# Down products by sevens in an MLP whose weights are unpacked on the way

## The chip, the cores and the metric

The kernel runs on one core of a Trainium2 chip. The metric is the device time of one execution in microseconds (us). Engines are named as in the profile: PE (TensorE, matrix products; PEld is its loading of weights), DVE (VectorE), ACT (ScalarE), POOL (GpSimd) and SP (SyncE, which here only issues DMAs).

## The reference

Two sequences of T = 1024 tokens with model width DM = 512 pass through two layers, everything in fp32. Each layer adds an attention and then an MLP to x, both on a layer norm of x: `x = x + attn0(ln(x)); x = x + mlp0(ln(x)); x = x + attn1(ln(x)); x = x + mlp1(ln(x))`. Attention 0 is a gated delta rule (a recurrence over tokens, computed in chunks of 128 tokens); attention 1 is a softmax attention through a small latent. MLP 0, where most of the change lies, has its weights as 4-bit codes with one scale for 32 values:

```
Wg = dequant(gate_W_packed, gate_scales)      # 4096 x 512, Wu alike; Wd 512 x 4096
gate, up = xt @ Wg.T, xt @ Wu.T
inter = gelu(gate) * up                       # tokens x 4096
out = inter @ Wd.T
```

MLP 1 is sparse (two of four hidden values are kept) and isn't touched.

## The kernel before

**Stages.** The two sequences are worked on half a step apart. `weave(main, fill)` (L157) interleaves the instructions of two generators: main says at each yield how much filling it wants (FILL = 3.3), fill says how much it has given (STEP = 3.4, or half of it for one product of seven). In the stage that the change acts in, main is the delta attention of sequence 1 (`delta.second`, 8 chunks of 128 tokens) and fill is MLP 0 of sequence 0 (`Unpacked.rest`). In the stage after it main is attention 1 of sequence 0 and fill is MLP 0 of sequence 1 (`Second.run`). The instruction order of PE, DVE, ACT and POOL is the order in which the program issues them; each engine works strictly through its own list. SP issues the DMAs in the same way.

**MLP 0, sequence 0 (`Unpacked`).** The 4096 hidden units are cut into NC0 = 8 chunks of 512. For each chunk six units of weights have to be unpacked: gate, up and down, each in halves. A unit (`unpack`) is three jobs: two times three DVE operations (two on the integer codes, L925 and L926, and a scaling product, L929), and then, for the gate and up units, four sums on POOL (L229 to L232), the store of the unpacked weights to DRAM (`kept`, for sequence 1) and the load of the codes of the unit two places further on (`codes.load`: one DMA of codes and eight of scales, L910 and L914). `plan` puts the jobs of units into a queue, and `core.spend(n)` issues n of them.

Chunks 0 and 1 (EARLY = 2) are done in plain products. In chunks 2 to 7 the gate and up products are done "by sevens": a 2 x 2 block product in seven block products instead of eight (`SEVEN`, in the order 1, 2, 6, 5, 7, 3, 4), with sums of blocks as factors (S1, S2, S3, S4 on the left from `left_sums`, T1 to T4 on the right from `right_sums`). One such set is a `macro`: seven products of two 128x512 matmuls (L1018). Products 1, 6 and 5 are copied out of PSUM by ACT into a tile `part` (L991), the others are added or multiplied in by DVE (L1036, L1048, L1052), and the second addend is put on with one product's delay. Two PSUM banks take the products in turn. An fp32 matmul is two rows in the profile's counts.

The down products of chunks 2 to 7 were plain: `outcome` goes over the 8 token tiles, multiplies four 128x512 matmuls into one bank (`o_ps`, the matmul itself is in a helper, L201), has DVE add the bank to x (L1161) and spends one unpacking job per tile. Jobs are also spent at each product of a macro. The order of units in later chunks was gate 0, up 0, down 0, gate 1, up 1, down 1: each macro planned one unit, and the down stretch two.

**MLP 0, sequence 1 (`Second`).** It reads the unpacked weights back, and does all three products by sevens, the down products too (`Seven.output`, `right_factors`, `left`; matmuls of 128x256, L1064, x adds L1079 on DVE and L1081 on POOL). Its pool of weights (`z_left`, two buffers) is opened in `open()`, after the first weave has ended, and its first weights are asked for there.

**x of sequence 0** is eight tiles of 128x512 (`Core.hold`), stored to DRAM (`park`, L1163) as each is finished in the last chunk. Attention 1's weights (L1369 to L1378) are loaded into the place of x, and its first work is to read the parked x back (`xl`, L1441).

**Delta attention, sequence 1.** Each chunk passes through `early` (prepare, solve), `late` (invert, advance) and `normed`. `fetch` loads its stored projections `cv` (a ring of 2) and its gate `gw` (a ring of 3) one slot ahead. The triangular inverse is a run of small DVE operations (`prod` L603, `inv` L604); `Ud` L693 and `o` L724 follow from PE results.

Of the kernel before, what the change touches and what calls it, by code (L numbers as in the profile page):

```python
# [81 lines left out]
class Core:  # L82
# [21 lines left out]
    def hold(self, pool, b):  # L104

        for n in range(b * TT, (b + 1) * TT):
            self.x[n] = pool.tile([P, DM], F32, tag=f"x{n}", name=f"x{n}")
# [146 lines left out]
class Delta:  # L254
# [570 lines left out]
    def second(self, stored, away, fill):  # L825
# [5 lines left out]
        def fetch(c):  # L831
            d = self.d[c]
            d["cv"] = self.ring("cv", [P, 3 * NG, P], 2)
            nc.sync.dma_start(out=d["cv"], in_=self.away[c][0])
            d["gw"] = self.ring("gw", [P, NH, DH], 3)
            nc.sync.dma_start(out=d["gw"], in_=self.away[c][1])
            d["beta"], d["g"] = self.late[:, c, :NH], self.late[:, c, NH:]
# [7 lines left out]
        def early(c):  # L845
            if c < CH:
                yield from self.prepare(c)
                yield
                yield
                yield from self.solve(c)  # L850

        def late(c):
            if 0 <= c < CH:
                x = self.d[c]["x"] = self.ring("x", [P, DM], 2)
                nc.sync.dma_start(out=x, in_=a["x"][(CH + c) * P : (CH + c + 1) * P, :])
                yield from self.invert(c)
# [16 lines left out]
        for slot in range(CH + 2):  # L873
            if slot + 1 < CH:
                fetch(slot + 1)
# [84 lines left out]
class Seven:  # L960
# [122 lines left out]

    def places(self, x, q):
# [7 lines left out]
class Unpacked(Seven):  # L1092
# [6 lines left out]
    def __init__(self, core, banks, codes, xT, kept, park):  # L1099
        super().__init__(core, banks, AF.Gelu_apprx_tanh, core.nc.vector)  # L1100
        self.codes, self.xT, self.kept, self.park = codes, xT, kept, park
# [4 lines left out]
        later = (("gate", 0), ("up", 0), ("down", 0), ("gate", 1), ("up", 1), ("down", 1))  # L1106
# [4 lines left out]
    def tile(self, u):  # L1111
# [3 lines left out]
        if w == "down":  # L1115
            t = self.wp.tile([P, 2, 512], F32, tag="w_down", bufs=3, name="w_down")
# [37 lines left out]
    def outcome(self, c, hs, tbs):  # L1154
# [3 lines left out]
        for n in range(4 * tbs[0], 4 * tbs[-1] + 4):  # L1158
            po = self.banks.one("o_ps")
            product(nc, po, [(h, wd[s // 2][:, s % 2, :]) for s, h in enumerate(hs(n))])  # L1160
            nc.vector.tensor_add(core.x[n], core.x[n], po)  # L1161
            if c + 1 == NC0:
                nc.sync.dma_start(out=self.park[n], in_=core.x[n])  # L1163
            core.spend(3 - len(tbs))
            yield STEP

    def chunk(self, c, tb, swap=None):
# [14 lines left out]
        if swap:  # L1182
            swap()
            self.plan(c + 1, ("gate", 0), ("up", 0))
        elif tb:
            self.plan(c + 1, ("gate", 1), ("up", 1), ("down", 0), ("down", 1))
        yield from self.outcome(
            c, lambda n: [h[:, s, n % 4 * P : n % 4 * P + P] for s in range(4)], (tb,)
        )
# [19 lines left out]
    def macro(self, c, half, w, g):  # L1209

        left = self.blocks(self.ws.pop((c, w, half)))
        for p in self.gate(left, g) if w == "gate" else self.up(left, g):
            self.step(p, 0)
            self.core.spend(1)
            yield STEP / 2
        self.core.spend()

    def rest(self):
# [5 lines left out]
        for c in range(self.EARLY, NC0):  # L1224
            gs = [self.wp.tile([P, 2, 2, T // 2], F32, tag=f"h{half}", name="h0") for half in range(2)]
            for (half, w), ahead in zip(
                ((0, "gate"), (0, "up"), (1, "gate"), (1, "up")),
                (("down", 0), ("gate", 1), ("up", 1), ("down", 1)),
            ):
                self.plan(c, ahead)  # L1230
                yield from self.macro(c, half, w, gs[half])
            self.step(4, 0)
            self.plan(c + 1, ("gate", 0), ("up", 0))
            yield from self.outcome(
                c,
                lambda n: [gs[s // 2][:, s % 2, n // 4, n % 4 * P : n % 4 * P + P] for s in range(4)],
                (0, 1),
            )
            core.spend()
# [3 lines left out]
class Second(Seven):  # L1243
# [4 lines left out]
    def __init__(self, core, banks, xT, x, kept, park):  # L1248
        super().__init__(core, banks, AF.Gelu_apprx_tanh, core.nc.gpsimd)
        self.x, self.kept, self.park = x, kept, park  # L1250
        self.tokens(xT, core.pools("g_x"), core.nc.vector)

    def open(self):
        self.wp = self.core.pools("g_w")
        self.tmp = self.core.pools("g_tmp")
        self.todo = [(c, w, half) for c in range(NC0) for half in range(2) for w in ("gate", "up")]
        self.ws = {self.todo[0]: self.weights(self.todo[0])}
        self.sums(self.todo[0])

    def weights(self, u):  # L1260
# [3 lines left out]
        t = self.wp.tile([P, 7, 2 * P], F32, tag="z_left", bufs=2, name="z_left")  # L1264
# [20 lines left out]
    def right_factors(self, wd):  # L1285
        half = DM // 2
        blocks = {
            f"{i + 1}{j + 1}": wd[:, 2 * i : 2 * i + 2, j * half : (j + 1) * half] for i in range(2) for j in range(2)
        }
        new = [self.wp.tile([P, 2, half], F32, name=f"wd_t{i}") for i in range(2, 5)]  # L1290
# [869 lines left out]
```

## Time and profile before

| | us |
|---|---|
| median of three runs | 3184.75 |
| lowest, highest | 3184.72, 3187.76 |
| profiled execution | 3184.22 |
| its span | 3182.5 |

The span is the stretch from the first to the last instruction of the profiled execution; some 1.7 us lie around it. Four windows of the trace give the stages (us; busy time of each engine in it, and the clock that the throttle granted to PE):

| window | length | PE | DVE | ACT | POOL | clock |
|---|---|---|---|---|---|---|
| 0 to 520: attention 0 of both, first MLP tokens | 520 | 462.18 | 365.15 | 202.90 | 139.88 | 0.94 |
| 520 to 1292: delta of sequence 1, MLP 0 of sequence 0 | 772 | 756.54 | 417.40 | 155.00 | 164.84 | 0.99 |
| 1292 to 2210: attention 1 of sequence 0, MLP 0 of sequence 1 | 918 | 909.88 | 570.54 | 307.99 | 279.64 | 0.99 |
| 2210 to the end: the rest | 972.5 | 952.04 | 609.84 | 267.25 | 155.19 | 0.98 |

A group's line in the profile reads: source line, engine, operation, output <- inputs by the program's names, shape, count | busy us, mean ns of one | idle time of the engine just before them, and what ended it. "<-DVE part L1052" behind an idle time means that the engine waited for that DVE operation. Matmuls overlap, so the mean ns of one is more than the pace from start to start. The chain of waits lists start, duration and what it was.

### The profile page before, as it was taken

How to read it: one execution, taken by the hardware profiler on the slowest of the kernel's cores; microseconds unless marked ns; L12 is line 12 of the kernel's file. 1: busy time of each engine (PE TensorE's matmuls, PEld its weight loads, DVE VectorE, ACT ScalarE, POOL GpSimd, SP SyncE). 2: the span in 40 equal slices, each digit the busy share in tenths (PEclk: the TensorE clock that was granted, in tenths of full speed). 3: DMA queues.
4: the chain of work that ended last, by engine and by line, in shares of the span. 5: the costliest groups of instructions: out<-in, count | busy, mean ns of one | idle time of the engine just before them, and what ended most of it. 6: DMA issues, size and time to landing. Idle time of an engine off the chain costs nothing.

```text
span 3182.5 us, 35790 instructions
## 1 busy us (share of the span) xinstructions
PE 3080.6 (97%) x13012; PEld 1624.7 (51%) x13012; DVE 1962.9 (62%) x3609; ACT 933.1 (29%) x1380; POOL 739.5 (23%) x790
## 2 busy tenths in 40 slices
PE   7899899999999999999999999999999999999998
PEld 6788654555555554454444354346433233334547
DVE  6787753366666555357567575655575577454766
ACT  4544311122121211221354114622202710442221
POOL 3333201122222211346312121222100700340000
PEclk9999999999999999999999999999999999999999
DMA  2111134132322224236301211123000020015211
GB/s 91 35 30 29 51 98 148 43 109 90 106 87 84 91 81 161 67 121 207 113 25 53 71 48 37 47 77 119 27 30 11 4 77 14 1 66 166 70 47 50
DMA packets 194784, 229.15 MB, mean 72 GB/s; under 512 B 53744, under 2 KB 148464, under 8 KB 194096
## 3 DMA queue, kind: packets, MB, share of 16 engines
q1 hardware_dynamic: 194608, 226.86, 22.3%
q8 instruction: 103, 1.69, 0.2%
q14 instruction: 73, 0.60, 0.1%
HBM read 154.16 MB, written 72.61 MB: 71 GB/s over the span
## 4 chain that ended last, share of the span: by engine, by line
PE 76%; DVE 5%; POOL 2%; issue 2%; DMA 1%; ACT 1%; SPq 0%; DVEq 0%; POOLq 0%; ACTq 0%
PE z_ps L1018 24%; PE o_ps L201 12%; PE z_ps L1064 8%; PE u_ps L201 5%; PE g_ps L201 5%; PE st_ps L1562 5%; PE av_ps L1593 4%; PE s_ps L1504 4%; PE den_ps L1615 1%; PE wide_ps L640 1%; PE small_ps L630 1%; PE hT_ps L1405 1%; PE small_ps L201 1%; PE wide_ps L397 1%; PE wide_ps L558 1%
## 5 line engine op out<-in xcount | busy, mean ns | idle before, releaser
L991 ACT COPY part<-z_ps 128x512 f32<-128x512 f32 x288 | 168.5, 585 | 738.3 <-PE z_ps L1018 501.5
L1018 PE MATMUL z_ps<-xT,z_left 128*128 128x512 f32 x768 | 359.7, 598 | 0.1
L1513 DVE TENSOR_REDUCE top<-s_ps 128x2 f32<-128x1024 f32 x256 | 301.0, 1217 | 77.5 <-PE s_ps L1504 77.4
L1018 PE MATMUL z_ps<-xt,z_left 128*128 128x512 f32 x576 | 274.9, 600 | 2.2 <-issue 1.0
L1573 ACT ACTIVATE es<-st_ps 128x1024 f32<-128x1024 f32 x214 | 209.9, 1022 | 129.5 <-PE st_ps L1562 124.4
L1018 PEld LDWEIGHTS z_ps<-xT,z_left 128*128 128x128 f32 x768 | 141.3, 190 | 187.6 <-issue 162.5
L201 PE MATMUL o_ps<-w_down,h 128*128 128x512 f32 x512 | 230.0, 600 | 0.4 <-DVE part L1052 0.4
L1018 PE MATMUL z_ps<-xT,w_left 128*128 128x512 f32 x384 | 182.0, 603 | 3.7 <-DVE part L1052 2.7
L1052 DVE TENSOR_TENSOR part<-z_ps,part 128x512 f32<-128x512 f32 x108 | 74.4, 689 | 174.1 <-PE z_ps L1018 168.5
L1018 PEld LDWEIGHTS z_ps<-xt,z_left 128*128 128x128 f32 x576 | 106.4, 191 | 147.3 <-issue 124.9
L1608 POOL TENSOR_TENSOR es<-es 128x512 f32<-128x512 f32 x96 | 132.5, 1408 | 148.5 <-PE av_ps L1593 144.9
L1562 PE MATMUL st_ps<-q,kT 17*128 17x512 f32 x1024 | 162.0, 657 | 1.7 <-ACT es L1573 1.7
L1504 PE MATMUL s_ps<-kT,q 16*128 16x512 f32 x1024 | 154.2, 640 | 4.9 <-DVE top L1513 4.8
L201 PEld LDWEIGHTS o_ps<-w_down,h 128*128 128x128 f32 x512 | 95.4, 191 | 110.7 <-issue 106.3
L201 PE MATMUL proj_ps<-xT,wqkv 128*128 128x256 f32 x576 | 135.2, 389 | 14.4 <-ACT gw L427 14.4
L1593 PE MATMUL av_ps<-es,v 128*32 128x512 f32 x1024 | 141.9, 626 | 0.0
L1018 PE MATMUL z_ps<-xt,w_left 128*128 128x512 f32 x288 | 137.8, 601 | 0.7 <-DVE part L1052 0.7
L1635 DVE TENSOR_TENSOR acc<-acc,es 128x1024 f32<-128x1024 f32 x96 | 131.8, 1420 | 0.0
L1053 POOL TENSOR_TENSOR h<-h,part 128x512 f32<-128x512 f32 x48 | 66.5, 1387 | 279.9 <-DVE part L1052 279.9
L201 PEld LDWEIGHTS proj_ps<-xT,wqkv 128*128 128x128 f32 x576 | 108.4, 193 | 33.6 <-ACT gw L427 17.6
L1036 DVE TENSOR_TENSOR h<-z_ps,part 128x512 f32<-128x512 f32 x84 | 57.9, 689 | 102.4 <-PE z_ps L1018 89.4
L1161 DVE TENSOR_TENSOR x<-x,o_ps 128x512 f32<-128x512 f32 x64 | 43.9, 686 | 122.3 <-PE o_ps L201 122.2
(316 smaller groups left out, 5317.0 us busy)
## 6 DMA issues: line engine op xcount, KB each, us to landing
sums<-factor SPq DMA_DIRECT2D x24, 512.0 KB, 3.4
kept_gate<-w_left SPq DMA_DIRECT2D x12, 896.0 KB, 3.8
kept_up<-w_left SPq DMA_DIRECT2D x12, 896.0 KB, 3.9
z_left<-kept_gate SPq DMA_DIRECT2D x12, 896.0 KB, 4.6
z_left<-kept_up SPq DMA_DIRECT2D x12, 896.0 KB, 4.5
kept_down<-w_down SPq DMA_DIRECT2D x16, 512.0 KB, 3.0
wd<-kept_down SPq DMA_DIRECT2D x16, 512.0 KB, 4.1
xl<-park SPq DMA_DIRECT2D x32, 256.0 KB, 2.9
```

The lines of the kernel that those rows point to most:

```text
L201: nc.tensor.matmul(ps, lhsT, rhs, start=(i == 0), stop=(i == len(pairs) - 1))
L991: self.core.nc.scalar.copy(t, src)
L1018: self.core.nc.tensor.matmul(ps, left[l][:, k, :], self.right[r][:, k, :], start=(first and k == 0), stop=(k == 1), skip_group_check=True,)
L1052: nc.vector.tensor_add(v, ps, v)
L1064: nc.tensor.matmul(ps[:, i * dm : (i + 1) * dm], left[l][:, k, i * P : (i + 1) * P], right[r][k], start=(first and i == 0 and k == 0), sto ...
L1504: nc.tensor.matmul(tiles[h4 // 2][:, h4 % 2 * 512 : h4 % 2 * 512 + 512], q1s[t][r : r + HALF, gr, :], kT[r : r + HALF, gr, j * 512 : (j + ...
L1513: nc.vector.tensor_reduce(top[:, j, h : h + 2], tiles[e].rearrange("p (i k) -> p i k", i=2), AX.X, ALU.max, negate=True)
L1562: nc.tensor.matmul(tiles[h4 // 2][h4 % 2], kT[r : r + CR, gr, kt * P : (kt + 1) * P], q2[r : r + CR, gr, :], start=True, stop=True,)
L1573: nc.scalar.activation(t.rearrange("p i q -> p (i q)"), tile[2], AF.Exp, scale=HALF**-0.5)
L1593: nc.tensor.matmul(av[gr][32 * h4 : 32 * h4 + 32, :], v[:, kt, 4 * gr + h4, :], es[u][h4 // 2][:, h4 % 2, :], start=(kt == 0), stop=(kt == ...
L1608: eng.tensor_add(t, t, es[u][h4 // 2][:, h4 % 2, :])
L1635: nc.vector.tensor_add(t, es[u - 1][e] if kt == 1 else t, es[u][e])
```

## The change

The down products of chunks 2 to 7 in `Unpacked` are done by sevens (`outputs`): two halves q of the tokens, each with seven products of four 128x256 matmuls, with left factors summed on DVE, right factors on POOL, three copies on ACT, and the x adds on DVE and POOL. No unpacking job is spent in them. Therefore the units come in the order gate 0, up 0, gate 1, down 0, up 1, down 1, and the four macros of a chunk plan one, two, two and one of them. A chunk's two down halves lie in one tile `wd`. The four right sums begin at product 3 of the last macro. x of sequence 0 becomes one tile of 128 x 8 x 512, since a place of an x add spans two token tiles, and its parks go out in two lots. In `Second` the pool for `z_left` is one of its own, opened with the object, and the first weights are asked for there. Delta's rings become one `cv` and two `gw`; the next `cv` is fetched after the first step of `prepare`, and `gw` in `late`.

```diff
@@ Core.hold
-        for n in range(b * TT, (b + 1) * TT):
-            self.x[n] = pool.tile([P, DM], F32, tag=f"x{n}", name=f"x{n}")
+        x = pool.tile([P, TT, DM], F32, name="x")
+        for n in range(TT):
+            self.x[b * TT + n] = x[:, n, :]
+        return x
@@ Delta.second
-            d["cv"] = self.ring("cv", [P, 3 * NG, P], 2)
+            d["cv"] = self.ring("cv", [P, 3 * NG, P], 1)
             nc.sync.dma_start(out=d["cv"], in_=self.away[c][0])
-            d["gw"] = self.ring("gw", [P, NH, DH], 3)
-            nc.sync.dma_start(out=d["gw"], in_=self.away[c][1])
...
-                yield from self.prepare(c)
+                steps = self.prepare(c)
+                next(steps)
+
+                if c + 1 < CH:
+                    fetch(c + 1)
+                yield
+                yield from steps
...
+                gw = self.d[c]["gw"] = self.ring("gw", [P, NH, DH], 2)
+                nc.sync.dma_start(out=gw, in_=self.away[c][1])
                 yield from self.invert(c)
...
-            if slot + 1 < CH:
-                fetch(slot + 1)
@@ Seven (moved here from Second)
+    def right_factors(self, wd, pool):
...
+        new = [pool.tile([P, 2, half], F32, tag=f"wd_t{i}", bufs=1, name=f"wd_t{i}") for i in range(2, 5)]
+        right = right_sums(self.core.nc.gpsimd, blocks, new)
...
+    def left(self, hs, q, calls, pool, again=False):
...
+        names = (1, 2) if again else (1, 2, 4)
+        new = [pool.tile([P, 2, HB], F32, tag=f"h_s{i}", bufs=1, name=f"h_s{i}") for i in names]
+        if again:
+            new.append(blocks["12"])
+        return left_sums(Recorder(self.core.nc.vector, calls), blocks, new)
@@ Unpacked
-        later = (("gate", 0), ("up", 0), ("down", 0), ("gate", 1), ("up", 1), ("down", 1))
+        later = (("gate", 0), ("up", 0), ("gate", 1), ("down", 0), ("up", 1), ("down", 1))
...
-        if w == "down":
-            t = self.wp.tile([P, 2, 512], F32, tag="w_down", bufs=3, name="w_down")
+        if w == "down" and c + 1 < self.EARLY:
+            t = self.plain.tile([P, 2, 512], F32, tag="w_down", name="w_down")
+        elif w == "down":
+
+            if half == 0:
+                self.wd = self.wp.tile([P, 4, 512], F32, tag="wd", name="wd")
+            t = self.wd[:, 2 * half : 2 * half + 2, :]
...
@@ Unpacked.macro
             self.core.spend(1)
+            if p == 3 and (half, w) == (1, "up"):
+                self.factors = self.right_factors(self.wd, self.sevens)
             yield STEP / 2
         self.core.spend()
+
+    def outputs(self, c, gs):
+
+        core, nc = self.core, self.core.nc
+        calls = deque()
+        left = self.left(gs, 0, calls, self.sevens, True)
+        for q in range(2):
+            for p in self.output(left, self.factors, self.places(self.x, q), nc.gpsimd):
+                self.step(p, 0)
+                if p == 1:
+                    while len(calls) > 1:
+                        calls.popleft()()
+                elif p == 6:
+                    calls.popleft()()
+                elif p == 4 and q == 0:
+                    left = self.left(gs, 1, calls, self.sevens, True)
+                elif p == 2 and q == 1:
+                    self.keep(c, 0)
+                yield STEP / 2
+        if c + 1 == NC0:
+            self.step(4, 0)
+            self.step(4, 0)
+            self.keep(c, 1)
+
+    def keep(self, c, q):
+
+        if c + 1 == NC0:
+            for n in (2 * q, 2 * q + 1, 4 + 2 * q, 5 + 2 * q):
+                self.core.nc.sync.dma_start(out=self.park[n], in_=self.core.x[n])
@@ Unpacked.rest
-                (("down", 0), ("gate", 1), ("up", 1), ("down", 1)),
+                (
+                    ((c, "up", 0),),
+                    ((c, "gate", 1), (c, "down", 0)),
+                    ((c, "up", 1), (c, "down", 1)),
+                    ((c + 1, "gate", 0),),
+                ),
             ):
-                self.plan(c, ahead)
+                for u in ahead:
+                    self.plan(u[0], u[1:])
                 yield from self.macro(c, half, w, gs[half])
-            self.step(4, 0)
-            self.plan(c + 1, ("gate", 0), ("up", 0))
-            yield from self.outcome(
-                c,
-                lambda n: [gs[s // 2][:, s % 2, n // 4, n % 4 * P : n % 4 * P + P] for s in range(4)],
-                (0, 1),
-            )
-            core.spend()
+            yield from self.outputs(c, gs)
@@ Second
         self.tokens(xT, core.pools("g_x"), core.nc.vector)
+        self.zp = core.pools("g_z")
+        self.todo = [(c, w, half) for c in range(NC0) for half in range(2) for w in ("gate", "up")]
+        self.ws = {self.todo[0]: self.weights(self.todo[0])}
 
     def open(self):
         self.wp = self.core.pools("g_w")
         self.tmp = self.core.pools("g_tmp")
-        self.todo = [(c, w, half) for c in range(NC0) for half in range(2) for w in ("gate", "up")]
-        self.ws = {self.todo[0]: self.weights(self.todo[0])}
         self.sums(self.todo[0])
...
-        t = self.wp.tile([P, 7, 2 * P], F32, tag="z_left", bufs=2, name="z_left")
+        t = self.zp.tile([P, 7, 2 * P], F32, tag="z_left", bufs=2, name="z_left")
```

## The prediction

> **What bounds the kernel now.** The first part of the page and the engine shares of the chain of waits come first.
>
> ```profile
> PE 3080.6 (97%) x13012; PEld 1624.7 (51%) x13012; DVE 1962.9 (62%) x3609; ACT 933.1 (29%) x1380; POOL 739.5 (23%) x790
> PE 76%; DVE 5%; POOL 2%; issue 2%; DMA 1%; ACT 1%; SPq 0%; DVEq 0%; POOLq 0%; ACTq 0%
> ```
>
> TensorE is busy 97% of the span and is 76% of the chain that ends last; everything else is small. The change acts in one stage, from about 520 to 1292 us (MLP 0 of sequence 0 woven into the delta attention of sequence 1), so that stage is read alone: its window, then its groups (busy, mean ns | idle before).
>
> ```profile
> 520.00:1292.00 772.00, 756.54 (x2944) 412.04 (x2943) 417.40 (x888) 155.00 (x250) 164.84 (x187) 0.99 0.31 98
> L201 PE MATMUL o_ps<-w_down,h 128*128 128x512 f32 x480 | 216.1, 600 | 0.4 <-DVE part L1052 0.4
> L1018 PE MATMUL z_ps<-xT,w_left 128*128 128x512 f32 x384 | 182.0, 603 | 3.7 <-DVE part L1052 2.7 <-DVE h L1036 0.5 <-DVE h L1048 0.5
> ```
>
> PE is busy 756.5 of 772 us (DVE 417, POOL 165), at clock 0.99. The plain down products (o_ps) never wait: 0.4 us idle in 480 rows. Fewer PE rows here are therefore time, unless new waits come with them. Where it waits is the other kind of product, sevens (z_ps L1018), on DVE's `part` and `h` adds. What a row costs is read from the chain of waits (start, us, what): a plain down stretch, and a stretch of sevens' down products from the MLP of sequence 1, which has them already.
>
> ```profile
> 1264.39 10.73 PE o_ps L201 x25
> 1379.17 3.46 PE z_ps L1064 x16
> ```
>
> 10.73/25 = 429 ns for a 128x512 row, 3.46/16 = 216 ns for a 128x256 row.
>
> **The change part by part.**
>
> *Down products, chunks 2 to 7.* Removed per chunk: 8 tiles x 4 fp32 products x 2 rows = 64 rows x 429 = 27.46 us. Added: 2 halves x 7 x 4 x 2 = 112 rows x 216 = 24.19 us. Gain 3.27 us a chunk, **-19.6 us** for six. The stage's 480 o_ps rows have a mean pace of 439 ns by their start times, so the 384 that go also take 384 x 10 ns = **-3.8 us** of small waits with them.
>
> *What the new products wait for.* Each half has four sums of h on DVE (0.684 us each by the L957 rows), three part copies on ACT (0.585), four x adds on DVE and three on POOL (1.26 to 1.39). Before, a tile had one 0.686 us add in 3.4 us. The third product, p6, needs S2, DVE's second sum, which can start only when the last up product p4 has been multiplied in. From the end of p4: multiply 0.68, S1 0.68, S2 0.68 and hand-over make about 2.9 us, against p1 and p2 (16 rows, 3.45 us): 0.5 us of slack. DVE works in order, though, and in the changed order of instructions the delta attention's triangular inverse (prod L603, inv L604: twelve of them took 647.03 to 650.87, some 3.4 us without the x add among them) stands ahead of S1 in chunk 2 and eight of its operations with `Ud` and `o` in chunk 5, `mix` (0.55) in chunk 4; in chunks 3, 6, 7 and in every second half nothing does. That makes p6 about 2 us late in chunk 2 and 1.5 in chunk 5. What such a lateness costs is in the trace where the MLP of sequence 1 had one (chain of waits):
>
> ```profile
> 1502.88 1.13 DVE h L957
> 1504.02 1.67 DVE h_s L957
> 1505.69 1.15 DVE top L1513
> ...
> 1509.14 5.33 PE z_ps L1064 x16
> ```
>
> PE stood for 1.89 us (1505.0 to 1506.9) and then paid 5.33 us for 16 rows instead of 3.46: the granted clock is 0.50 from 1509.1 to 1512.5. **A rule beside this row:** the Trainium skill, "TensorE: Matmul & The Clock Gate", "What's actually happening" and "HAM oscillation", halves the clock after an idle window of 3.4 us and calls only gaps above that harmful; by it the two stalls cost 2 + 1.5 = 3.5 us. By the row a pause of 1.9 us is followed by one half-speed window, 1.7 us more each: 6.9 us. I take the row, **+6.9**. As a cross-check, the woven sevens of sequence 1 (1375.08: 3.65 us for 16 rows; 1383.70: 1.94 for 8) run 228 to 242 ns; 10 ns over 216 on 672 rows would be 6.7 us.
>
> **A second rule, against the change:** "SBUF — State Buffer", "SBUF: two separate sides", says that a DVE operation with two SBUF inputs and a GpSimd operation that reads SBUF take turns on one shared port pair, the loser blocked for the whole instruction. The left sums are such operations, and the four right sums of POOL, started after the sixth of the last up macro's seven products (4 x 1.39 = 5.6 us), run just then. DVE rows of the second half of a chunk of sequence 1:
>
> ```profile
> 1391.65 0.84 DVE L957 TENSOR_TENSOR h_s<-h,h 128x512 f32<-128x512 f32 x1
> 1392.53 1.10 DVE L957 TENSOR_TENSOR h_s<-h_s,h 128x512 f32<-128x512 f32 x1
> 1393.55 1.21 DVE L957 TENSOR_TENSOR h<-h 128x512 f32<-128x512 f32 x1
> 1394.68 1.75 DVE L957 TENSOR_TENSOR h_s<-h,h_s 128x512 f32<-128x512 f32 x1
> ```
>
> They stretch to 1.75 while POOL's 0.73 us operations stretch to 1.17, so the trace agrees that the two hinder each other. By the rule's worst case each of S1 and S2 waits out a 1.39 us sum, p6 is 2.3 us late in all six chunks, +14 us and more; by the row S1 + S2 take 1.94 instead of 1.37, which eats the 0.5 us of slack and little else. I take the row: **+1**.
>
> *Unpacking.* Unchanged in work: 24 gate and up units and 12 down units, each 0.42 + 0.43 + 0.69 us of DVE twice, the former with 2.9 us of POOL sums. The down stretch carried one 1.54 us job per tile; now none. Macro (0,"up") carries gate 1 and down 0, (1,"gate") up 1 and down 1. A unit's last job issues the codes of the unit two further on: nine DMAs of 0.42 to 0.55 us on SP, about 4 us, landing 2.5 (at most 5.7) us later. Counting PE's rows between that job and the first use, the lead was 18 to 39 us and becomes 9 to 20, against the 6.5 to 10 needed; DVE waited 0.5 us in all for codes before. Bound: -0 to +12 (2 us in each chunk); two chunks come out short by up to 2 us: **+2**. Two units in one macro double DVE's load there (7 products x 1.7 us of PE, about 12 us, with 6 x 1.54 = 9.2 us of jobs and the delta's own work), where the `part` adds already hold PE. L1018's idle 3.7 + 0.7 us over 24 macros is the lower end, twice that in the twelve heavier ones the upper: **+4**.
>
> *DVE elsewhere.* The 3.68 us wait of L703 on `Ud` at 653.5, followed by some 10 us at clock 0.5, has unpacking ahead of it in DVE's order (651.84, 652.30). One unit leaves that place: 1.54 us sooner. **-3**, between -7 (no half-speed windows) and 0.
>
> *POOL.* 24 right sums and 36 x adds are new: 60 x 1.39 = 83 us on an engine busy 165 of 772. They go ahead of the delta's short operations (L117 2.3, L519 1.8 us), which PE waits for through DVE: **+2**, 0 to +6.
>
> *Delta rings.* cv has one buffer and gw two; both are fetched later, but still most of a slot (some 90 us of stage) before use. Nothing; if that cover were gone, one landing (2.9 us for xl's 256 KB) for each of 8 chunks.
>
> *The passage at 1292.* Parks of x leave in two lots, the last after POOL's final add; x0 is now one tile, so the attention's weights (wlat and four more), that take its place, wait for all parks instead of one each. On SP they are in order ahead of the second xl, which was read by DVE 6.4 us after the end of the MLP and now about 10.6; behind its statistics stands p7's add, for which PE waits about 2 us, 3.7 with a half-speed window: **+3**. The weights of "a place of their own" come to nothing: their load was issued at 1252.9 before, well ahead of 1292.
>
> *Sum:* -19.6 - 3.8 + 6.9 + 1 + 2 + 4 - 3 + 2 + 3 = **-7.5**. The profiled execution took 3184.22 (span 3182.5 and 1.7 around it), the median 3184.75, so 3176.7 for the profiled one and **3177** for the median.
>
> **Rivals.**
>
> *Clean gain.* The stalls fit the slack or fall where PE has the delta's rows to do: -19.6 - 3.8 + 4 = -19: **3165**. For it: o_ps hardly waits now; against it: L1064 waits in sequence 1 although it is placed the same way.
>
> *Wash.* The new waits are twice what I charge (each chunk has one 2 us stall with its half-speed window, 6 x 3.7 = 22): **3184**. For it: DVE is in order and the inverse comes in bursts; against it: the clean order in four chunks.
>
> *Slower, by one mechanism:* two units packed into one macro. Codes come late, DVE (in order) stands at the unpacking, and the z_ps adds behind it hold the two banks and PE. Without it the sum is -13.5, so over six chunks it takes the gain at 2.3 us a chunk and makes the kernel slower by 0.2% from 3.3. One landing 2.7 us late with its half-speed window is 4.4 a chunk, +26: **3198**. For it: lead halved; against: only 2 of 6 chunks short by the count.
>
> *Not doing what it says:* the weights' own place, as shown above, worth nothing; it changes no number.
>
> **How the numbers follow.** About 0.2% (6.4 us) is what a measurement tells from no change. Forecast case (3168 to 3181) 0.46, of which 0.06 within 0.2%; clean 0.14; wash 0.21; slower 0.19. Faster 0.54, same 0.27, slower 0.19. The range 3162 to 3196 takes in all but the far end of the slower case and a gain beyond the rows' own.
>
> **What would show it.** L1064 in 520:1292 with 672 rows at 216 to 230 ns; idle before it on `h_s` L957, largest in chunks 2 and 5; `part` L1052 idle in macros above 4.4 us; codes waits on DVE near 2 us; POOL 165 to about 250; the stage's end at 1279 to 1288 instead of 1291.9. The forecast is wrong if p6 waits in every chunk, or if L1018 loses over 10 us more.

## The result

The changed kernel is slower: 3191.33 us against 3182.98 (medians of 20 runs each), a ratio of 1.0031 with a 95% interval of 1.0022 to 1.0039, about +10 us. The forecast was 3177, faster. Single runs of either kernel spread over some 12 to 14 us, so the ratios below, which carry intervals, say more than one profiled execution.

The profiled executions took 3184.22 before and 3189.71 after (+5.5). Cut at the same instructions in both: the stage from the first plain down product of its fill to the first product of the next MLP took 763.5 us before (528.2 to 1291.7) and 771.6 after (526.0 to 1297.6), **+8.1**; the passage into the next stage cost 2.8 more; what follows, whose instructions are the same in both, was 3.4 shorter and what lies before the stage about 2 shorter in this execution, which is the spread just told. The stage itself hardly spreads: a kernel with nothing but other rings (e4, below) and one with only other tiles of x (e3) took 765.0 in it (before: 763.5) and 768.5 (changed: 771.6). So the loss is where the change is. The first part of the page and the stage's window, after:

```profile
PE 3071.6 (96%) x13300; PEld 1681.7 (53%) x13300; DVE 2020.7 (63%) x3657; ACT 953.6 (30%) x1416; POOL 830.5 (26%) x850
```

```profile
520.00:1298.00 778.00, 746.07 (x3226) 468.34 (x3225) 475.17 (x935) 175.12 (x285) 251.96 (x241) 0.98 0.30 93
```

PE is busy 9 us less in all and the span is 5.4 us longer: work went, as it was to, and waiting more than took its place. In the stage DVE has gone from 417 to 475 us, POOL from 165 to 252. The stage's groups show where (lines have moved: L1018 is L1024 now, L1052 is L1058, the down products L1070). The second group of gate and up products before the change, and the groups after it:

```profile
L1018 PE MATMUL z_ps<-xt,w_left 128*128 128x512 f32 x288 | 137.8, 601 | 0.7 <-DVE part L1052 0.7
...
L1024 PE MATMUL z_ps<-xT,w_left 128*128 128x512 f32 x384 | 187.7, 617 | 8.2 <-DVE part L1058 5.2 <-DVE h L1042 1.6 <-ACT h L1039 0.7
L1024 PE MATMUL z_ps<-xt,w_left 128*128 128x512 f32 x288 | 139.2, 606 | 4.2 <-DVE part L1058 4.2
L1070 PE MATMUL z_ps<-wd,h 128*128 128x256 f32 x288 | 68.4, 386 | 1.3 <-DVE x L1085 1.0 <-DVE h L963 0.3
L1070 PE MATMUL z_ps<-wd_t,h 128*128 128x256 f32 x192 | 46.1, 383 | 2.2 <-DVE x L1085 2.2
```

The gate and up products, which the change doesn't touch, wait 8.2 + 4.2 us where they waited 3.7 + 0.7 before. From start to start their 672 rows took 324.3 us instead of 307.7: **+16.6**. The down products' 672 rows took 158.3 us; the 384 plain rows they replace took 169.0: **-10.7**, where the rows alone give -23.4. The rest of the +8.1 are the delta's rows, 2.1 us longer. Time at a granted clock of 0.50 in the stage went from 13.7 to 27.3 us; what it costs is part of these sums.

Cut by macro, the loss of the gate and up products is the time that their rows took above 429 ns each (us, six chunks; e1, e2 and e10 are experiments told below):

| kernel | gate 0 | up 0 | gate 1 | up 1 |
|---|---|---|---|---|
| before: one unit in each | 8.3 | 3.3 | 3.4 | 4.4 |
| changed: two in up 0 and gate 1 | 8.9 | 10.6 | 6.4 | 10.1 |
| e2: before, with these two packed | 6.4 | 7.8 | 7.6 | 21.6 |
| e1: changed, one unit in each | 16.1 | 7.2 | 2.8 | 3.8 |
| e10: e1, jobs kept off the inverse | 14.5 | 2.6 | 2.8 | 3.0 |

Of the 16.6 us, 10.3 lie in the macros that carry two units now, and 5.7 in up 1, which carries one as before.

What the longest wait is made of shows in the timeline of the changed kernel, macro up 0 of chunk 4 (start, us, engine and line, what; in brackets the idle time ahead and what ended it):

```profile
907.09 0.72 DVE L717 TENSOR_TENSOR S<-S,small_ps 64x192 f32<-64x192 f32 x2 [3.25 <-POOL S L711]
907.84 0.56 DVE L728 TENSOR_TENSOR o<-o,small_ps 128x384 f32<-128x384 f32 x1
908.31 0.35 DVE L605 TENSOR_TENSOR prod<-inv,blk 48x121 f32<-48x121 f32 x1
...
910.86 0.41 DVE L931 TENSOR_SCALAR nib<-codes 128x512 int32<-128x512 int32 x1
911.31 0.43 DVE L932 TENSOR_SCALAR nib<-nib 128x512 int32<-128x512 int32 x1
911.77 0.69 DVE L935 SCALAR_TENSOR_TENSOR wd<-nib,codes 128x512 f32<-128x512 fp8e4 x1
912.38 0.68 DVE L1058 TENSOR_TENSOR part<-z_ps,part 128x512 f32<-128x512 f32 x1
912.98 0.42 DVE L931 TENSOR_SCALAR nib<-codes 128x512 int32<-128x512 int32 x1
913.12 2.97 PE L1024 MATMUL z_ps<-xt,w_left 128*128 128x512 f32 x4 [4.21 <-DVE part L1058]
```

The add `part` has been possible since PE's rows of 907.0 ended near 908.9, at the latest. DVE first idles 3.25 us for the delta's `S`, which POOL makes only after four weight sums of the unpacking (903.4 to 906.6); then come `o`, a part of the inverse (908.3 to 910.9) and an unpacking job of w_down, which before the change did not lie in this macro. PE stands 4.21 us, and the granted clock is 0.50 from 914.0 to 920.8 (2.97 us for four rows).

### The profile page after: what moved, and what is told of

Read it like the earlier page. It is cut to its first block, busy times and chain, and to the rows that moved or that the text cites. A ratio compares the mean times of both kernels' runs of the same rounds, so it can differ in the third digit from the quotient of the medians.

```text
span 3187.9 us, 36603 instructions
## 1 busy us (share of the span) xinstructions
PE 3071.6 (96%) x13300; PEld 1681.7 (53%) x13300; DVE 2020.7 (63%) x3657; ACT 953.6 (30%) x1416; POOL 830.5 (26%) x850
## 4 chain that ended last, share of the span: by engine, by line
PE 53%; DVE 3%; POOL 2%; issue 1%; DMA 1%; ACT 0%; SPq 0%; DVEq 0%; POOLq 0%
PE z_ps L1024 16%; PE z_ps L1070 9%; PE o_ps L203 5%; PE st_ps L1606 5%; PE av_ps L1637 4%; PE s_ps L1548 4%; PE u_ps L203 4%; PE g_ps L203 3%; PE den_ps L1659 1%; DMA sums<-factor 1%; PE hT_ps L1449 1%; PE lat_ps L203 1%; PE kv_ps L1514 0%; DMA wo<-in_wo 0%; PE ln_ps L151 0%
## 5 line engine op out<-in xcount | busy, mean ns | idle before, releaser
L997 ACT COPY part<-z_ps 128x512 f32<-128x512 f32 x324 | 189.6, 585 | 850.5 <-PE z_ps L1024 489.9
L1024 PE MATMUL z_ps<-xT,z_left 128*128 128x512 f32 x768 | 360.7, 599 | 0.1
L1024 PE MATMUL z_ps<-xt,z_left 128*128 128x512 f32 x576 | 275.1, 600 | 5.8 <-DVE h L1042 3.6
L1617 ACT ACTIVATE es<-st_ps 128x1024 f32<-128x1024 f32 x214 | 209.9, 1022 | 125.7 <-PE st_ps L1606 120.5
L1024 PEld LDWEIGHTS z_ps<-xT,z_left 128*128 128x128 f32 x768 | 141.8, 191 | 188.3 <-issue 162.9
L1024 PE MATMUL z_ps<-xT,w_left 128*128 128x512 f32 x384 | 187.7, 617 | 8.2 <-DVE part L1058 5.2
L1087 POOL TENSOR_TENSOR x<-x,part 128x512 f32<-128x512 f32 x84 | 117.9, 1405 | 279.2 <-DVE x L1085 269.2
L1024 PEld LDWEIGHTS z_ps<-xt,z_left 128*128 128x128 f32 x576 | 105.9, 190 | 150.9 <-issue 124.2
L1058 DVE TENSOR_TENSOR part<-z_ps,part 128x512 f32<-128x512 f32 x108 | 74.3, 689 | 149.9 <-PE z_ps L1024 144.0
L1024 PE MATMUL z_ps<-xt,w_left 128*128 128x512 f32 x288 | 139.2, 606 | 4.2 <-DVE part L1058 4.2
L1085 DVE TENSOR_TENSOR x<-x,z_ps 128x512 f32<-128x512 f32 x112 | 76.3, 683 | 99.0 <-PE z_ps L1070 97.6
L1070 PE MATMUL z_ps<-wd,h 128*128 128x256 f32 x544 | 129.3, 386 | 1.3 <-DVE x L1085 1.0
```

What stands on the lines that cost most here:

```text
L997: self.core.nc.scalar.copy(t, src)
L1024: self.core.nc.tensor.matmul(ps, left[l][:, k, :], self.right[r][:, k, :], start=(first and k == 0), stop=(k == 1), skip_group_check=True,)
L1070: nc.tensor.matmul(ps[:, i * dm : (i + 1) * dm], left[l][:, k, i * P : (i + 1) * P], right[r][k], start=(first and i == 0 and k == 0), sto ...
L1087: self.soon.append(lambda x=x, v=parts[{2: 1, 7: 5, 3: 6}[p]]: adder.tensor_add(x, x, v))
L1617: nc.scalar.activation(t.rearrange("p i q -> p (i q)"), tile[2], AF.Exp, scale=HALF**-0.5)
```

## The experiments

Two theories came from these rows. **A:** DVE works its list in order, and PE waits for the z_ps adds that stand behind unpacking and inverse; packing two units into one macro is the cause. **B:** the down products' own sums and adds are. Two more concern one place each: **C** the passage into the next stage, **P** POOL's load. Times are told as the ratio to the kernel before, run on the same chip beside each; the changed kernel has 1.0031, and 0.001 is 3.2 us. Each kernel has one trace.

### Packing, taken back and put alone (e1, e2)

e1 is the changed kernel with the old order of units:

```diff
-        later = (("gate", 0), ("up", 0), ("gate", 1), ("down", 0), ("up", 1), ("down", 1))
+        later = (("gate", 0), ("up", 0), ("down", 0), ("gate", 1), ("up", 1), ("down", 1))
@@ outputs
+        self.plan(c + 1, ("gate", 0), ("up", 0))
...
+                if p in (5, 3, 4):
+                    core.spend(1)
...
```

> The changed kernel with the unpacking laid out as before the change: one unit in each macro, two beside the down products (six jobs in fourteen products); the down products stay by sevens. Theory A (packing): two units in one macro make DVE late for the z_ps adds, and this is most of the loss; the L1018-type excess over 429 ns per row falls from 36 us back to about 20, the time falls by 8 to 14 us against the changed kernel (to 3178 to 3183). Theory B (the outputs' own waits): the left sums and x adds, behind the inverse on DVE, are the loss, and six more jobs beside them add to it: no gain or up to 6 us slower than the changed kernel.

Measured: 1.0014 (1.0005 to 1.0022), 5.4 us faster than the changed kernel, less than A's 8 to 14, and still slower than before. In the macros, PE's waits on `part` and `h` are 6.1 us in its trace (11.0 in the changed kernel, 4.4 before). But two units lie beside the down products again, their x adds come late, and PE waits 5.3 us for these at the head of the next gate 0, so that the gate and up rows regain only 6.2 of the 16.6 us.

e2 is the kernel before with the four macros planning one, two, two and one units and none beside the plain down products:

> The kernel before with only the unpacking packed as in the change (two units in the macros up 0 and gate 1, none beside the plain down products). Theory A: 8 to 14 us slower than before. Theory B: within 2 us of before.

Measured: 1.0081 (1.0065 to 1.0097), **+26 us**, twice what A expected. Its waits of PE (what waited <- for what: us in total, times, longest):

```profile
PE z_ps L1018 <- DVE part L1052: 16.2, 8, 4.2
```

Before the change the same line of that view is

```profile
PE z_ps L1018 <- DVE part L1052: 3.4, 4, 1.0
```

In these rows it loses 24.0 us. So the new order of units is dear by itself, but not only because two units load DVE: 17.2 of the 24.0 lie in up 1, which carries one unit. The order also brings the loads of codes closer to their use, and DVE stood 18.2 us for codes in this stage (0.5 before, 7.3 in the changed kernel). In up 1 of e2's chunk 6, for example, SP sends the codes behind the loads of the inverse, DVE stands at the unpacking, the add `part` waits behind it and PE for that:

```profile
1165.49 0.56 SPq L910 DMA_DIRECT2D codes<-in_pk_gate  x1
...
1168.41 0.43 DVE L925 TENSOR_SCALAR nib<-codes 128x512 int32<-128x512 int32 x1 [5.79 <-DMA codes<-in_pk_gate]
...
1171.63 0.69 DVE L929 SCALAR_TENSOR_TENSOR w_left<-nib,codes 128x512 f32<-128x512 fp8e4 x1 [2.33 <-DMA codes<-in_sc_gate]
...
1172.98 1.71 PE L1018 MATMUL z_ps<-xT,w_left 128*128 128x512 f32 x2 [2.88 <-DVE part L1052]
```

The longest of the waits on `part`, 4.2 us at 1278.0, stands behind a wait of DVE for another load (`xT`, 4.0 us), others behind the inverse. The four kernels together show more: without packing, sevens make the kernel 4.5 us slower (1 to 1.0014); with it, 16 us faster (1.0081 to 1.0031). What the down products gain or lose depends on what DVE has to do elsewhere. DVE's busy time by kind of stretch (chunks 2 to 7, summed over six) puts a number to it. "PE lost" is what the product rows took from start to start above 429 or 216 ns, with the idle time ahead of the delta's rows:

| kernel | macros: DVE us of us | PE lost | down: DVE us of us | PE lost |
|---|---|---|---|---|
| before | 260.2 of 416.6 (62%) | 21.9 | 114.6 of 227.2 (50%) | 6.9 |
| e2, plain, packed | 301.4 of 442.2 (68%) | 47.0 | 85.9 of 228.8 (38%) | 7.9 |
| e1, sevens, spread | 278.2 of 435.3 (64%) | 33.0 | 163.9 of 208.1 (79%) | 13.7 |
| changed: sevens, packed | 304.1 of 441.9 (69%) | 40.0 | 129.1 of 209.9 (61%) | 14.0 |

The plain down stretch was the place where DVE's work cost nothing: at 50%, the delta's inverse and a job per tile included, it lost no more than e2's at 38%. By sevens it loses 14, and the macros lose more than before in all three variants.

### DVE lighter (e5, e6)

Two integer operations of the unpacking are made one, in both kernels:

```diff
-            nc.vector.tensor_scalar(t, codes, 28 - 4 * i, 2, ALU.logical_shift_left, ALU.arith_shift_right)
-            nc.vector.tensor_scalar(t, t, 0x9C000000 - (1 << 32), None, ALU.bitwise_and)
+            nc.vector.tensor_scalar(t, codes, 28 - 4 * i, 0x9C000000 - (1 << 32), ALU.logical_shift_left, ALU.bitwise_and)
```

> The changed kernel with two of the integer operations of the unpacking made one (a shift and a mask, without the arithmetic shift between, so the weights' values are not the reference's): 0.43 us of DVE less for each half unit, 31 us less in chunks 2 to 7, nothing else moved. Theory A (PE waits for DVE's adds, which stand in order behind unpacking and the inverse): 12 to 20 us faster than the changed kernel. Theory P (POOL's right sums and the shared port hold DVE and delta): less than 6 us faster.

> The same leaving-out in the kernel before (values as in e5). Theory A: 3 to 8 us faster than before, less than the changed kernel gains, since the plain down products hide DVE's work. Theory P: 3 us or less.

Measured: 0.9963 (0.9948 to 0.9977) and 0.9971 (0.9960 to 0.9983). That is 22 us for the changed kernel and 9 for the one before, a little more than A expected of either; but the edit reaches chunks 0 and 1 too, ahead of the stage, where the traces are 5.7 and 2.9 us shorter (only the first is outside of the spread of the kernels that leave this part alone, 523.4 to 529.6). The stage alone, by the traces, went from 771.6 to 759.5 us in the changed kernel (-12.1) and from 763.5 to 760.6 before (-2.9). So 31 us less of DVE buy two times (by the runs) to four times (by the stage) as much where the down products are by sevens and the macros are packed, though PE's rows are the same. This is as A says, and with DVE this much lighter the change no longer loses.

### POOL lighter (e7)

```diff
-                self.factors = self.right_factors(self.wd, self.sevens)
+                half = DM // 2
+                b = lambda i, j: [self.wd[:, 2 * i + k, j * half : (j + 1) * half] for k in range(2)]
+                self.factors = {
+                    "11": b(0, 0), "21": b(1, 0), "22": b(1, 1), "T1": b(0, 1), "T2": b(0, 0), "T3": b(1, 0), "T4": b(1, 1)
+                }
```

> The changed kernel without the right sums of chunks 2 to 7 (the blocks of w_down stand in their place, so the down products of these chunks are not the reference's): 24 POOL operations of 1.4 us less. Theory P: 6 to 10 us faster than the changed kernel. Theory A: within 2 us of it.

Measured: 1.0006 (0.9996 to 1.0017), 8 us faster than the changed kernel, the intervals apart, and within P's 6 to 10. The trace doesn't bear P out, though. The pause in the passage into the next stage is gone here, which makes the passage 3.8 us shorter, and this needn't have to do with POOL's load (see the passage, below). The stage is 6.1 us shorter, but not by fewer waits: DVE still stands 3.25 us for `S` in chunk 4, since the sums ahead of it are the unpacking's; PE waits 12.0 us on `part` and `h` in the macros (11.0 in the changed kernel) and 3.5 for T (3.0). What is shorter is the time at half speed behind such waits, 13.7 instead of 27.3 us, and it differs between executions with the same waits too (20.5 in e3). POOL does slow DVE: the four left sums take 0.90, 0.88, 0.77 and 0.79 us in the mean in the changed kernel (0.68 alone), and 0.86, 0.72, 0.68 and 0.79 here. What the right sums' work on POOL costs is not shown by this run.

### The sums beside the down products (e14, e15)

On e1, so with the unpacking spread, the left sums are left out (the blocks of h are the factors), then the right ones as well.

```diff
+        if again:
+            calls.extend([lambda: None] * 4)
+            b = blocks
+            return {
+                "11": b["11"], "12": b["12"], "22": b["22"], "S1": b["21"], "S2": b["22"], "S3": b["21"], "S4": b["12"]
+            }
         return left_sums(Recorder(self.core.nc.vector, calls), blocks, new)
```

> The kernel of e1 with the left sums of chunks 2 to 7 left out (blocks of h stand in their place, so these down products are not the reference's): 48 DVE operations of 0.69 us less, 33 us. If DVE's load beside the down products takes the gain: 8 to 14 us faster than e1. If POOL's load does: within 3 us of e1.

> The kernel of e14 with the right sums of these chunks left out too (24 POOL operations of 1.4 us). If DVE alone matters: as e14 within 2 us. If POOL delays delta's short operations or DVE through the shared port: 5 to 9 us faster than e14.

Measured: 0.9991 (0.9979 to 1.0003) and 0.9971 (0.9954 to 0.9987). The 33 us of left sums cost some 7 us (just under the range for DVE), so B has its share beside A. Leaving out the right sums gave some 6 more, though the intervals of e14 and e15 overlap a little; in the traces the stage is the same (760.9 and 761.0 us), and e15 gains by the pause in the passage, which it lacks like e7. Even without any sum the kernel is only 9 us faster than before, where the rows give 23. The largest waits left that weren't there before are for the x adds: PE waits 4.5 + 4.0 us for them in e15's trace, behind inverse and unpacking.

### The inverse in finer parts (e8)

```diff
-        for rows in (range(1, 7), range(7, 11), range(11, 14), range(14, 16)):
+        parts = (range(1, 7), range(7, 11), range(11, 14), range(14, 16))
+        if self.b:
+            parts = (range(1, 6), range(6, 9), range(9, 11), range(11, 13), range(13, 15), range(15, 16))
+        for rows in parts:
```

> The changed kernel with the inverse of sequence 1 given out in six parts of 10, 6, 4, 4, 4 and 2 DVE operations instead of four of 12, 8, 6 and 4. Theory A, with bursts of the inverse as the cause: 4 to 8 us faster than the changed kernel. If the total load of DVE in the macros is the cause and not the bursts, or theory P: within 2 us.

Measured: 1.0078 (1.0065 to 1.0092), +15 us over the changed kernel. The reason shows in PE's waits in the stage, first lines:

```profile
PE small_ps L635 <- DMA T<-dT: 26.2, 3, 11.4
PE z_ps L1027 <- DVE h L1045: 7.1, 5, 2.9
```

Six parts end two yields of the program later than four. The inverse goes to DRAM and comes back as T, and PE, which works in order too, came to T's product before the load had landed, up to 11.4 us. The waits on `part` shrank, from 9.4 to 2.1 us, those on `h` grew from 1.6 to 7.1. The edit mixed two things, so it settles nothing about the bursts; these were tried another way.

### Unpacking steps aside (e10, e12)

```diff
@@ Delta.solve, after each part of the inverse
+            self.core.burst = 1
             yield
@@ Unpacked.macro
             self.step(p, 0)
-            self.core.spend(1)
+            if not self.core.burst:
+                self.core.spend(1)
+            self.core.burst = 0
...
```

> The kernel of e1 with no unpacking job given out at the product that follows a part of the inverse (it comes at the next product, or at the macro's end). Theory A with coincidence (an unpacking job of 1.5 us on top of some 2 us of inverse makes the z_ps add miss its turn): PE's waits on part and h in the macros fall by half or more, 4 to 8 us faster than e1. If only the total load counts: within 2 us of e1.

> The kernel before with the rule of e10 in its macros. Theory A with coincidence: 1 to 4 us faster than before (its macros lose 22 us in all, of which the part and h waits are 4 to 5). Else within 2 us.

Measured: e10 0.9995 (0.9986 to 1.0004), 6 us faster than e1; e12 0.9990 (0.9982 to 0.9999), 3 us faster than before. Nothing is computed less; only the order on DVE differs. e10's gain is in its trace as well (stage 756.9 us, e1 763.1). e12's is not: its stage took 763.7 where before took 763.5, the waits on `part` and `h` fell by 1 us only, and e4 (below), of which nothing was expected, measured 0.9992. So e12 doesn't show a gain. The macros' waits of PE in e1:

```profile
PE z_ps L1024 <- DVE part L1058: 4.3, 3, 2.4
...
PE z_ps L1024 <- DVE h L1042: 1.8, 2, 1.5
```

and in e10:

```profile
PE z_ps L1026 <- DVE part L1060: 0.7, 1, 0.7
...
PE z_ps L1026 <- DVE h L1044: 0.3, 1, 0.3
```

So in e1, with one unit in each macro, it is the coincidence of a part of the inverse and a job that makes PE late for these adds, rather than DVE's total. The rule was not tried with the packed order. The x waits of the down products (13.1 us, `z_ps <- DVE x`) stayed.

e13 put the same rule into the down products (on e11, below):

> The kernel of e11 with the same rule in the down products: no unpacking job at a product that follows a part of the inverse. Theory A with coincidence: the 12 us that PE waits for x adds in and behind the down products (2.8 and 4.9 us the longest) fall by half, 4 to 7 us faster than e11. If these waits come from the left sums and x adds themselves: within 2 us of e11.

Measured: 0.9999 (0.9989 to 1.0008), against e11's 0.9986: no gain. PE's waits for x fell from 12.0 to 6.4 us and those for the left sums rose from none to 4.3: the jobs that were put off met S1 and S2. Here putting them off moved the wait and did not remove it.

### Rings, tiles of x, and the passage (e3, e4, e9, e11)

e4 is before with only delta's ring changes of the change; e3 is the changed kernel with

```diff
-        x = pool.tile([P, TT, DM], F32, name="x")
+        pairs = [pool.tile([P, 2, DM], F32, tag=f"x{m}", name=f"x{m}") for m in range(TT // 2)]
...
```

> The kernel before with only the rings of delta changed (one cv, two gw, fetched later). Theories A, B and C: within 2 us of before. A rival (the later fetches put DMAs into SP's queue ahead of the inverse's T loads): 3 us or more slower than before, with PE waiting for T.

> The changed kernel with x of sequence 0 in four tiles of two token tiles each instead of one, so that attention 1's weights wait for two parks each and not for all eight. Theory C (the passage at 1292 to 1298 costs 5.5 us by a 3.8 us wait of PE and a half-speed window): 3 to 5 us faster than the changed kernel, and the 3.65 us wait on h falls under 1.5. Theories A and B: no change beyond 1 us, since what PE loses there is given back later in the stage after.

Measured: e4 0.9992 (0.9983 to 1.0001), so the rings cost nothing; e3 1.0022 (1.0012 to 1.0032), which the intervals don't tell from the changed kernel, and its trace still has PE's pause, 3.2 us, at the same instruction, where C expected under 1.5. The passage of the changed kernel:

```profile
1305.69 0.42 SPq L1343 DMA_DIRECT2D wd<-kept_down  x1
1306.21 7.29 SPq L1485 DMA_DIRECT2D xl<-park  x4
...
1310.38 0.69 DVE L128 BATCH_NORM_STATS2 ln_st<-xl 128x6 f32<-128x512 f32 x1 [4.64 <-DMA xl<-park]
...
1311.40 1.29 DVE L1042 TENSOR_TENSOR h<-z_ps,part 128x512 f32<-128x512 f32 x2
...
1312.14 2.65 PE L1024 MATMUL z_ps<-xt,z_left 128*128 128x512 f32 x4 [3.65 <-DVE h L1042]
```

The second xl is issued only at 1306.2, 8.6 us after the MLP's end, DVE waits for it with the z_ps add `h` behind, and PE for that. By e3 the reason is not one tile instead of eight. e9 is e1 with the last chunk's down products plain, so that x is parked tile by tile again; e11 joins e9 and e10.

> The kernel of e1 (sevens, unpacking spread as before the change) with the down products of the last chunk plain again, its x parked tile by tile, x in four tiles. Theory C (the passage into the next stage loses 4 to 5 us by late parks, whatever the tiles of x are): the 3.4 us wait behind ln_ps goes; 1 to 3 us faster than e1, though 3.3 us of rows come back. If the passage is given back later in the next stage: 2 to 3 us slower than e1.

> e9 and e10 together. Theories A with coincidence and C: 6 to 10 us faster than e1, so 2 to 6 us faster than before. Otherwise as e9 or e10.

Measured: e9 1.0012 (1.0001 to 1.0022), the pause gone, the time as e1's, where C expected 1 to 3 us less. That x is finished late, as C has it, is not the reason either. The pause (3.2 to 4.3 us, after which PE is 5.1 to 6.6 us behind; in the changed kernel 2.8 of them remain) stands in the changed kernel, e1, e3, e5, e8, e10 and e14. It is missing in e7 and e15, whose last down products are by sevens and whose x is parked in the same two lots. These two have no right sums in the last chunk, and neither has e9. In e7 SP sends the next MLP's `wd` more than 20 us earlier than above, and three xl ahead of attention 1's weights where the changed kernel has one:

```profile
1272.77 0.94 SPq L1347 DMA_DIRECT2D wd<-kept_down  x2
...
1296.42 1.69 SPq L1489 DMA_DIRECT2D xl<-park  x3
1298.96 0.33 SPq L1417 DMA_DIRECT2D wlat<-in_wlat  x1
```

So the right sums of the last chunk, or the place of their tiles `wd_t`, hold up the loads of the passage; which of the two was not tried.

e11 0.9986 (0.9979 to 0.9993): **faster than both kernels**, 4.5 us under before. How much of this the sevens give is open: by the runs its interval overlaps that of e12, which has no sevens in these down products (0.9990); by the traces the stage is 759.3 us in e11, 763.7 in e12 and 763.5 before.

## Why the prediction was wrong

By the traces, stage and passage came to +8.1 + 2.8 = +10.9 us where the sum said -7.5. Of these 18.4 us, 12.6 lie in the gate and up products and 4.8 in the down products.

- *Down products.* The rows were priced rightly (429 and 216 ns, both at the median again). Net of waits they were to give -19.6 - 3.8 + 6.9 + 1 = -15.5; they gave -10.7.
- *What they wait for.* I had S2 late in chunks 2 and 5 (+6.9). PE waited 0.6 us for `h_s` in all. The waits were for x adds (4.0 us directly) and, in the delta's rows between them, for T (3.0): DVE and SP behind, at places other than the one I had followed.
- *Two units in one macro, "+4".* **This is the step that failed**: the term for what the new order of units costs the gate and up products was mis-sized, 16.6 us where it said 4. I took L1018's 4.4 us of idle time over 24 macros as the lower end of what heavier macros add and its double in twelve as the upper. But those 4.4 us are what PE waited with DVE busy 62% of the macros, and say nothing of 69%; besides, by start times the rows had lost 19.4 us before, not 4.4. What the runs show in its place: DVE comes to the z_ps adds too late, and PE's waits on `part` and `h` in the macros follow the order of DVE's work, 4.4 us before, 11.0 in the changed kernel, 19.4 in e2, 6.1 in e1, 1.0 in e10. e2 shows that the new order of units does it without any sevens in the down products (+24.0 in these rows, +26 in all), and e5 that DVE is the engine (9.8 us less in these rows with 31 us less of DVE). Two units in one macro are only a part of it: 10.3 of the 16.6 us lie in these macros, 5.7 in up 1. The rival "slower, two units packed into one macro" came by its sign (3198; it was 3191), and so did the sign that I had named for being wrong, that L1018 loses over 10 us more. Its path came in part: in the changed kernel DVE waited 4.9 and 2.4 us for the codes of one unit, at 939 and 942, and PE 1.7 us for `mix` behind it; ahead of the longest wait DVE stood for `S` and then had other work. In e2 late codes had a larger part (18.2 us of DVE's waiting).
- *Earlier L703 wait, -3.* As told: the pause that ended at 653.5 went from 3.7 to 2.2 us (it ends at 649.9 now), and the half-speed time behind it from 10.2 to 6.8. The second half may be chance: in e4, with the pause of 3.7 us, it was 6.8 too.
- *POOL, +2.* Not settled: e7 and e15 take the right sums away, but with them the pause in the passage.
- *Port rule.* I took the row against the rule's worst case. Where S1 and S2 met right sums, in chunks 3 and 4, the two took 3.28 and 2.93 us instead of 1.37, between the row's 1.94 and the 4.15 of the rule's worst case. In chunks 2, 5, 6 and 7 they met none and took 1.37 to 1.39. So the mean of the left sums is only 0.83 us, and PE hardly waited for them: the +1 was about right because they seldom met, which I had not argued.
- *Passage, +3.* 2.8 by the trace; the mechanism (the second xl, the add behind its statistics) as told, the tile of x as its reason wrong (e3), and I had no thought of the right sums' tiles. *Rings* and *a place of their own*: nothing, as told; the latter was not tried alone.
- *Clock.* Each pause of 2 us or more in the stage (2.2, 2.3, 3.0 and 4.2 us) brought half-speed time, and only the last is above 3.4 us: as the row had it. (The row's own 1.89 us stall was for `top`, not for a sum.) Two pauses of 4.2 and 1.6 us at 909 to 918 brought 6.8 us.

What stays open: of the 23 us that the rows save, e15 shows some 9 after all sums are gone; how the remaining loss divides between x adds, part copies and the shifted phase of the delta against the chunks was not separated. Nor was how much of the loss in the packed macros is DVE's load and how much the later codes.

## What to carry to other kernels

Work that a helper engine does beside an unhurried stretch of the bound engine is paid for when that stretch is made dense: before trading rows for sums, add up the helper's busy time by stretch, not over the span, and look for the stretch that served as its slack. On in-order engines place can matter as much as amount: keeping a 1.5 us job from following a 2 us burst (e10) gave 6 us with the same work, leaving out 33 us of sums (e14) gave 7. When a part is left out to see what it costs, look in the trace where the time went: here a good third of what the right sums seemed to cost (e7) lay in another stage. And when moving work, test the move alone with the old arithmetic (e2) before crediting the arithmetic.

## What the runs showed of the hardware

Every half-speed stretch in the changed kernel's stage (granted clock 0.50) lasts 3.4 or 6.8 us. The waits just ahead of them are of 0.77 (1149.4) to 4.21 us (913.1), while others of 1.32 (822.1), 1.35 (1244.4) and 1.67 (944.3) brought none: the length of one pause does not decide it. Nor does it decide how long the clock stays down: the same pause of 3.68 us for `Ud` was followed by 10.2 us at 0.50 in the kernel before and in e12, and by 6.8 in e1, e4 and e10.

A sum on DVE and one on POOL that run at the same time stretch each other. Two rows of the changed kernel:

```profile
832.12 1.59 POOL L242 TENSOR_TENSOR wd<-wd 128x512 f32<-128x512 f32 x1
832.63 1.64 DVE L963 TENSOR_TENSOR h_s<-h,h 128x512 f32<-128x512 f32 x1
```

The right sum on POOL takes 1.26 us alone and took 1.59; the left sum on DVE takes 0.68 alone, took 1.64, and ended 0.55 us after POOL's. By these numbers most of it was still to do when POOL's was through.
